# A transformer block pair at its start: the context columns as one array, the second token tile loaded directly behind the first, one square root for both

## The chip, the cores and the metric

The kernel runs on 1 core of one Trainium2 chip. The metric is the device time of one execution in microseconds (us). A core has TensorE (PE, with its weight loads PEld), VectorE (DVE), ScalarE (ACT), GpSimd (POOL) and SyncE (SP), which here only issues transfers.

## The reference

The inputs are x (8 batches of 100 tokens, 512 wide), a context ctx_512 (8 x 361 x 128) and the weights of two layers. In short:

```python
x = x + L0_xattn(layernorm(x), ctx_512, ...)   # 16 heads of 32, causal mask, softmax
x = x + L0_ffn(layernorm(x), ...)              # 8 experts, top 2 of them, silu gate
x = x + L1_xattn(layernorm(x), ctx_512, ...)   # latent attention with rotary tables
x = x + L1_ffn(layernorm(x), ...)              # rows rounded to 255 levels, silu gate

def L0_xattn(q, latent_kv, Wq, Wkv_expand, Wout):
    qp = q @ Wq.T
    k, v = jnp.split(latent_kv @ Wkv_expand.T, 2, axis=-1)
    ...
    scores = jnp.where(causal, scores, jnp.finfo(scores.dtype).min)
    attn = jax.nn.softmax(scores, axis=-1)
    ...
    return out @ Wout.T
```

The causal mask is lower triangular over 100 queries and 361 context rows, so that the first attention only ever sees the first 100 context rows of a batch. The change lies in the first attention alone.

## The kernel before

The 800 tokens lie in seven tiles of 128 rows (the last has 32), `xs[0]` to `xs[6]`. The kernel goes through the first attention batch by batch (0 to about 110 us), the choice of experts and the folding of some weights beside it (to about 140 us), the eight experts (to about 261 us), the second attention (to about 485 us) and the quantised feed-forward (to the end).

What the change touches is the start of the first attention, lines 193 to 288 and 465 to 475.

**Transfers.** At the start all are issued by SyncE, in the order in which they are written (L194 to L211, then the weights to be folded). They run on the same 16 DMA engines. `load_x(t)` brings one token tile, 256 KB. `wkv_sb` holds the weights of keys (first half) and values (second half), 256 KB each. `ctx0` holds the context's columns, 128 latent channels on the partitions and 8 x 100 rows along them, in two halves of four batches and 200 KB each (L198, L204). They are cut out of an array of 128 x 8 x 361 in HBM, so a partition's half is four pieces of 100 numbers (400 B). `wq_sb` holds the queries' weights, 1024 KB. The order before is x0, keys' weights, first context half, x1, wq, x2, x3, values' weights, second context half, x4 to x6, wout. From the ninth transfer on, each issue waits for the landing of the one eight places ahead of it, since eight semaphores are used in turn.

**Order of the engines.** From L249 TensorE, VectorE and ScalarE work in the order in which the program is written; nothing is moved by a scheduler there. An engine takes its instructions strictly in that order and waits at each for what it needs.

**The steps.** Three matmuls of zeros (L466) come first on TensorE. `first_norm(t0, t1)` takes mean and variance of the tiles t0 to t1-1 (L267, L268, VectorE), one square root over all of them (L271, ScalarE), one reciprocal (L272) and then a normalisation of each tile (L277), both on VectorE. `token_columns(t, xn)` transposes a tile's four blocks on TensorE (L286) and copies them to `xnT` (L287, ScalarE). `keys(h, o0, o1)` computes for four batches the key blocks o0 to o1-1 (L257, two passes each, TensorE) and copies them to `kT` (L261, ScalarE). `queries0(0, 2)` (L302, L306) needs the columns of tiles 0 and 1 and `wq_sb`. `first_norm(2, NT)` then treats the other five tiles together. `begin(0)` takes the scores of the first batch (L323, L329) and their maxima (L341, VectorE). The order before:

```python
    first_norm(0, 1)
    take_columns(0)
    first_norm(1, 2)
    keys(0, 0, 3)
    take_columns(1)
    keys(0, 3, KC)
    queries0(0, 2)
    first_norm(2, NT)
```

The first use of a function such as the square root on ScalarE is preceded by the loading of its table; this instruction is put in when the program is built and has the line of the instruction that it serves.

Of the kernel before, what the change touches and what calls it, by code (L numbers as in the profile page):

```python
# [19 lines left out]
P = 128  # L20
B, S, D = 8, 100, 512
N = B * S
L, DC = 361, 128
KC = D // P
# [26 lines left out]
def tile_kernel(  # L51
# [7 lines left out]
    nc = tc.nc  # L59
# [19 lines left out]
    def bank(dtype=F32):  # L79
        cols = 512 if dtype == F32 else 1024  # L80
        bank_turn[0] += 1
        pool = bank_pools[bank_turn[0] % len(bank_pools)]
        return pool.tile([P, cols], dtype, tag="bank", name="bank")
# [103 lines left out]
    ctx0 = ate.tile([P, B, S], F32, tag="ctx0", name="ctx0")  # L187
    wkv_sb = ate.tile([P, 2 * D], F32, tag="wkv", name="wkv_sb")
    wq_sb = ate.tile([P, KC, D], F32, tag="wq", name="wq_sb")
    xnT = ate.tile([P, KC, N], F32, tag="xnT", name="xnT0")  # L190
    wout_sb = at.tile([P, KC, D], F32, tag="wout", name="wout_sb")

    def load_x(t):
        nc.sync.dma_start(xs[t][: ROWS[t]], x[ds(t * P, ROWS[t]), :])  # L194

    load_x(0)
    nc.sync.dma_start(wkv_sb[:, :D], wkv0[:, :D])
    nc.sync.dma_start(ctx0[:, : B // 2], ctx_t[:, : B // 2, 0:S])  # L198
    load_x(1)
    nc.sync.dma_start(wq_sb, wq0.rearrange("(c p) o -> p c o", p=P))  # L200
    load_x(2)
    load_x(3)
    nc.sync.dma_start(wkv_sb[:, D:], wkv0[:, D:])
    nc.sync.dma_start(ctx0[:, B // 2 :], ctx_t[:, B // 2 :, 0:S])  # L204
    for t in range(4, NT):
        load_x(t)
    nc.sync.dma_start(wout_sb, wout0.rearrange("(c p) o -> p c o", p=P))
# [46 lines left out]
    def keys(h, o0=0, o1=KC):  # L254
        for o in range(o0, o1):
            pk = bank()
            nc.tensor.matmul(  # L257
                pk[:, :HALF], wkv_sb[:, ts(o, P)],
                ctx0[:, ds(h * 4, 4), :], start=True, stop=True,
            )  # L260
            nc.scalar.copy(kT[:, o, ts(h, HALF)], pk[:, :HALF])  # L261

    def token_stats(mvs, t0, t1):
        for t in range(t0, t1):
            r = ROWS[t]
            stats = small.tile([P, 6], F32, tag="stats", name="stats")
            nc.vector.bn_stats(stats[:r], xs[t][:r])  # L267
            nc.vector.bn_aggr(mvs[:r, t, :], stats[:r])  # L268

    def token_scales(mvs, sds, rstds, t0, t1):  # L270
        nc.scalar.activation(sds[:, t0:t1], mvs[:, t0:t1, 1], AF.Sqrt, bias=ln_eps)  # L271
        nc.vector.reciprocal(rstds[:, t0:t1], sds[:, t0:t1])  # L272

    def token_norm(t):
        r = ROWS[t]
        xn = ate.tile([P, D], F32, tag="xn0", name=f"xn0_{t}", bufs=NT)
        nc.vector.tensor_scalar(  # L277
            xn[:r], xs[t][:r], mv0[:r, t, 0:1], rstd0[:r, t : t + 1], ALU.subtract, ALU.mult
        )
        return xn  # L280

    def token_columns(t, xn):
        r = ROWS[t]
        pt = bank().rearrange("p (c q) -> p c q", c=KC)
        for c in range(KC):
            nc.tensor.transpose(pt[:, c, :r], xn[:r, ts(c, P)], ident[:r, :r])  # L286
        nc.scalar.copy(xnT[:, :, ds(t * P, r)], pt[:, :, :r])  # L287


    def queries0(b, n, parts=(0, 1)):  # L290
        per = 4 // n
        if parts[0] == 0:
            qT = atw.tile([P, KC, n * S], F32, tag=f"qT{n}", name=f"qT{b}")
            for i in range(n):
                queries_of[b + i] = qT[:, :, ts(i, S)]
                halves_of[b + i] = qT
        qT = halves_of[b]
        for o0 in [per * i for i in parts if per * i < KC]:
            pq = bank()
            for o in range(o0, o0 + per):  # L300
                for c in range(KC):
                    nc.tensor.matmul(  # L302
                        pq[:, ds((o - o0) * n * S, n * S)], wq_sb[:, c, ts(o, P)],
                        xnT[:, c, ds(b * S, n * S)], start=(c == 0), stop=(c == KC - 1),
                    )
            nc.scalar.activation(  # L306
                qT[:, ds(o0, per), :], pq[:, : KC * S].rearrange("p (c q) -> p c q", c=per),
                AF.Copy, scale=1.0 / math.sqrt(HD0),
            )
# [113 lines left out]
    queries_of, halves_of, soft, vals, xn0 = {}, {}, {}, {}, {}  # L423

    def first_norm(t0, t1):
        token_stats(mv0, t0, t1)
        token_scales(mv0, sd0, rstd0, t0, t1)
        for t in range(t0, t1):
            xn0[t] = token_norm(t)
# [5 lines left out]
    def take_columns(*tiles):  # L435
        for t in tiles:
            token_columns(t, xn0.pop(t))
# [26 lines left out]

    for _ in range(3):
        nc.tensor.matmul(bank()[:, :384], zeros[:, :P], zeros[:, :384], start=True, stop=True)  # L466
    first_norm(0, 1)
    take_columns(0)
    first_norm(1, 2)
    keys(0, 0, 3)  # L470
    take_columns(1)
    keys(0, 3, KC)
    queries0(0, 2)
    first_norm(2, NT)

# [533 lines left out]
    with tc.If(spills > 0, preferred_fallthrough_block=True):  # L1009
# [38 lines left out]
        with tc.For_i(0, NE, 1, hint_engines=()):  # L1048
# [12 lines left out]
            with tc.For_i(0, NT, 1, hint_engines=()):  # L1061
# [4 lines left out]
                pt = bank()  # L1066
# [661 lines left out]
    pt = bank()  # L1728
# [334 lines left out]
```

## Time and profile before

| what | us |
|---|---|
| the three timed runs | 624.87, 624.99, 627.96 (median 624.99) |
| the profiled execution | 624.9 |
| its span, from the first to the last instruction | 622.7 |
| TensorE busy in it | 601.0 (97%) |
| VectorE, ScalarE, GpSimd busy | 403.5, 231.8, 238.8 |

Times in the profile's rows count from the start of the span. A row of the order of time has start, duration, engine, line, operation, result and operands with their shape, and how many instructions were taken together; the brackets tell how long the engine had been idle before it and what ended that. SPq rows are issues of transfers, not the transfers. A row of the costliest groups has the count, the busy time in all and the mean in ns, then the idle time just before and what ended it. A row of waits has the total, the number and the longest.

These rows are the ones in which transfers are issued at the start (SPq), of which the prediction speaks:

```profile
0.79 0.39 SPq L194 DMA_DIRECT2D x<-in_x  x1
1.24 0.42 SPq L197 DMA_DIRECT2D wkv_sb<-in_wkv  x1
1.71 0.43 SPq L198 DMA_DIRECT2D ctx<-in_ctx_t  x1
2.18 0.51 SPq L194 DMA_DIRECT2D x<-in_x  x1
2.73 0.43 SPq L200 DMA_DIRECT2D wq_sb<-in_wq  x1
```

### The profile page before, as it was taken

What the parts mean: (1) busy time and instruction counts of PE and PEld (TensorE: products, weight loads), DVE (VectorE), ACT (ScalarE), POOL (GpSimd) and SP (SyncE); (2) the same over time, 40 slices, a digit from 0 to 9 for tenths busy, and PEclk for the clock granted to TensorE, in tenths of its full rate; (3) what the DMA queues carried; (4) which work ended last, traced back from release to release, by engine and by line L of the source; (5) the groups of instructions that cost most, each with busy time, mean ns of one, the idle gap of its engine ahead of it and who ended that gap; (6) DMA issues with size and microseconds to landing.
All of it is one profiled execution on the core that took longest, in us unless ns stands there. A gap on an engine that the chain in (4) does not pass through costs nothing.

```text
span 622.7 us, 12244 instructions
## 1 busy us (share of the span) xinstructions
PE 601.0 (97%) x4587; PEld 399.4 (64%) x4594; DVE 403.5 (65%) x1041; ACT 231.8 (37%) x533; POOL 238.8 (38%) x242
## 2 busy tenths in 40 slices
PE   8999999979999999999999999999999999999995
PEld 5767765647777777658877677777777544444442
DVE  4865778836777554253227888788874366766687
ACT  3553545561111111241336545556553121222130
POOL 1131231021333332208954868688685001222020
PEclk9999999999999999999999999999999999999998
DMA  8900096558999999773623332433210401110221
GB/s 279 326 20 35 2 298 182 179 155 255 306 301 268 233 329 308 201 197 102 180 67 86 91 101 53 127 88 88 59 50 6 139 10 32 24 31 11 53 41 68
DMA packets 92932, 83.75 MB, mean 134 GB/s; under 512 B 41195, under 2 KB 69567, under 8 KB 92743
## 3 DMA queue, kind: packets, MB, share of 16 engines
q1 hardware_dynamic: 88775, 73.57, 41.3%
q0 software_dynamic: 4096, 9.38, 7.3%
q8 instruction: 37, 0.61, 0.4%
q14 instruction: 24, 0.20, 0.1%
HBM read 63.75 MB, written 12.36 MB: 122 GB/s over the span
## 4 chain that ended last, share of the span: by engine, by line
PE 69%; DVE 5%; ACT 2%; issue 1%; POOL 1%; ACTq 0%; DVEq 0%
PE bank L390 13%; PE bank L1191 12%; PE four L1531 11%; PE bank L1497 8%; PE bank L1614 7%; PE bank L1252 7%; PE bank L1789 3%; PE bank L1292 2%; PE four L1461 2%; PE bank L1128 1%; PE four L1558 1%; ACT e L1505 1%; DVE sq L1522 1%; POOL hid L1806 1%; PE bank L396 1%
## 5 line engine op out<-in xcount | busy, mean ns | idle before, releaser
L1515 POOL TENSOR_SCALAR e<-e,rs 128x361 f32<-128x361 f32 x96 | 113.0, 1192 | 41.1 <-DVE rs L1511 40.8
L390 PE MATMUL bank<-wvo,ctxT 128*128 128x512 f32 x192 | 84.4, 594 | 0.0
L1505 ACT ACTIVATE e<-bank,nm 128x361 f32<-128x361 f32 x100 | 56.5, 567 | 51.6 <-DVE rs L1511 43.5
L1191 PE MATMUL bank<-xgT,w 128*128 128x240 f32 (+1 forms) x384 | 74.1, 369 | 0.4 <-ACT xgT L1132 0.4
L1191 PEld LDWEIGHTS bank<-xgT,w 128*128 128x128 f32 (+1 forms) x384 | 64.7, 181 | 11.5 <-issue 6.2
L1502 DVE TENSOR_REDUCE nm<-bank 128x1 f32<-128x361 f32 x100 | 50.8, 509 | 27.1 <-PE bank L1497 19.0
L1531 PEld LDWEIGHTS four<-sq,kv 32*128 32x128 f32 (+1 forms) x1536 | 62.2, 185 | 8.4 <-issue 4.8
L1497 PE MATMUL bank<-kvT,qe 128*128 128x361 f32 x192 | 67.3, 483 | 0.2
L1531 PE MATMUL four<-sq,kv 32*128 32x192 f32 (+1 forms) x1536 | 66.9, 325 | 0.0
L1806 POOL TENSOR_TENSOR hid<-g,u 128x512 f32<-128x512 f32 (+1 forms) x17 | 20.4, 1216 | 112.1 <-ACT g L1797 110.5
L390 PEld LDWEIGHTS bank<-wvo,ctxT 128*128 128x128 f32 x192 | 36.0, 190 | 42.5 <-issue 41.8
L1522 DVE STREAM_TRANSPOSE sq<-e 128x384 f32<-128x384 f32 x96 | 53.6, 558 | 1.6 <-POOL e L1515 0.8
L1264 POOL DMA_INDIRECT x_acc<-y,place x16 | 25.1, 1570 | 75.6 <-ACT y L1263 45.1
L355 POOL TENSOR_TENSOR s<-s,rs 100x800 f32<-100x800 f32 x16 | 24.4, 1522 | 70.3 <-DVE rs L354 35.5
L1497 PEld LDWEIGHTS bank<-kvT,qe 128*128 128x128 f32 x192 | 33.4, 189 | 22.6 <-issue 5.7
L1252 PE MATMUL bank<-w,hT 128*128 128x512 f32 (+3 forms) x96 | 42.6, 593 | 0.0
L1614 PE MATMUL bank<-xT,wqf 128*128 128x256 f32 (+1 forms) x128 | 31.2, 394 | 0.0
L1252 PEld LDWEIGHTS bank<-w,hT 128*128 128x128 f32 (+3 forms) x96 | 17.0, 183 | 19.7 <-issue 15.6
L1789 PE MATMUL bank<-w1q,xqT 128*128 128x512 bf16 (+1 forms) x140 | 29.2, 361 | 0.2
L1614 PEld LDWEIGHTS bank<-xT,wqf 128*128 128x128 f32 x128 | 23.8, 190 | 5.3 <-issue 0.5
L1794 DVE SCALAR_TENSOR_TENSOR g<-bank,sx,swb 128x512 f32<-128x512 f32 (+1 forms) x18 | 12.6, 702 | 19.0 <-PE bank L1789 18.5
L1202 ACT ACTIVATE silu<-bank 128x240 f32<-128x240 f32 x16 | 5.9, 370 | 50.1 <-PE bank L1191 50.1
(296 smaller groups left out, 961.5 us busy)
## 6 DMA issues: line engine op xcount, KB each, us to landing
w<-in_w SPq DMA_DIRECT2D x8, 1408.0 KB
gu<-in_wgu SPq DMA_DIRECT2D x22, 256.0 KB
wq_p<-in_wq SPq DMA_DIRECT2D x8, 512.0 KB
w<-in_w SPq DMA_DIRECT2D x16, 256.0 KB
wo<-in_wo SPq DMA_DIRECT2D x8, 512.0 KB
kq_p<-in_wkcq SPq DMA_DIRECT2D x16, 192.0 KB
kv<-ctx_rot SPq DMA_DIRECT2D x32, 96.0 KB
dn<-in_wdn SPq DMA_DIRECT2D x4, 704.0 KB
```

What stands on the lines that cost most here:

```text
L390: nc.tensor.matmul(po[:, :D], lhs[:, c, ds(t * P, r)], rhs[:, c, :], start=(c == 0), stop=(c == chunks - 1),)
L1191: nc.tensor.matmul(po, w12_e[:, c, cols], xgT[:, c, :], start=(c == c0), stop=(c == c1 - 1))
L1252: nc.tensor.matmul(py[i][:n], hT[:mr, m, ds(s0, n)], w3_e[:mr, m, :], start=(m == blocks[0]), stop=(m == blocks[2]),)
L1497: nc.tensor.matmul(ps[:, :L], of_batch(b)[a][:, h, s].rearrange("p g q -> p (g q)"), kvTs[b], start=True, stop=True,)
L1502: nc.vector.tensor_reduce(nm, ps[:, :L], AX.X, ALU.max, negate=True)
L1505: nc.scalar.activation(e[:, :L], ps[:, :L], AF.Exp, bias=nm, accum_out=sm)
L1515: nc.gpsimd.tensor_scalar_mul(e[:, :L], e[:, :L], rs)
L1522: nc.vector.transpose(squares[b, h][:, a * (HT // 2) + s, :], e)
L1531: nc.tensor.matmul(pc[:, g, :cols].rearrange("p (t q) -> p t q", q=32), kv4s[b, j // NBH][ds(32 * g, n), j % NBH, :], eT[ds(32 * g, n), :, ...
L1614: nc.tensor.matmul(pq[:, i, :], wqf[:, c, ts(p0 + i, P)], xT[:, c, :], start=(c == 0), stop=(c == KC - 1),)
L1789: nc.tensor.matmul(pw[:r, :n], xqT[:, c, :r], w1q[:, c, ds(off, n)], start=(c == 0), stop=(c == KC - 1),)
L1806: nc.gpsimd.tensor_tensor(hid[:r, ds(c0, n)], g[:r, :n], u[:r, :n], ALU.mult)
```

## The change

The host hands over the context's columns already cut to the first 100 rows of each batch, so that a half of `ctx0` is one run of 400 numbers (1600 B) on each partition of the array in HBM. The transfer of x1 stands directly behind that of x0. The means, variances and the square root of tiles 0 and 1 are taken together. On TensorE two key blocks now come first, then the transposes of both tiles, then the other two key blocks. The copy of the second tile's columns is done by VectorE.

```diff
--- before.py
+++ after.py
@@ -194,14 +194,14 @@
         nc.sync.dma_start(xs[t][: ROWS[t]], x[ds(t * P, ROWS[t]), :])
 
     load_x(0)
+    load_x(1)
     nc.sync.dma_start(wkv_sb[:, :D], wkv0[:, :D])
-    nc.sync.dma_start(ctx0[:, : B // 2], ctx_t[:, : B // 2, 0:S])
-    load_x(1)
+    nc.sync.dma_start(ctx0[:, : B // 2], ctx_t[:, : B // 2])
     nc.sync.dma_start(wq_sb, wq0.rearrange("(c p) o -> p c o", p=P))
     load_x(2)
     load_x(3)
     nc.sync.dma_start(wkv_sb[:, D:], wkv0[:, D:])
-    nc.sync.dma_start(ctx0[:, B // 2 :], ctx_t[:, B // 2 :, 0:S])
+    nc.sync.dma_start(ctx0[:, B // 2 :], ctx_t[:, B // 2 :])
     for t in range(4, NT):
         load_x(t)
     nc.sync.dma_start(wout_sb, wout0.rearrange("(c p) o -> p c o", p=P))
@@ -279,12 +279,12 @@
         )
         return xn
 
-    def token_columns(t, xn):
+    def token_columns(t, xn, copy=nc.scalar.copy):
         r = ROWS[t]
         pt = bank().rearrange("p (c q) -> p c q", c=KC)
         for c in range(KC):
             nc.tensor.transpose(pt[:, c, :r], xn[:r, ts(c, P)], ident[:r, :r])
-        nc.scalar.copy(xnT[:, :, ds(t * P, r)], pt[:, :, :r])
+        copy(xnT[:, :, ds(t * P, r)], pt[:, :, :r])
 
 
     def queries0(b, n, parts=(0, 1)):
@@ -464,12 +464,11 @@
 
     for _ in range(3):
         nc.tensor.matmul(bank()[:, :384], zeros[:, :P], zeros[:, :384], start=True, stop=True)
-    first_norm(0, 1)
-    take_columns(0)
-    first_norm(1, 2)
-    keys(0, 0, 3)
-    take_columns(1)
-    keys(0, 3, KC)
+    first_norm(0, 2)
+    keys(0, 0, 2)
+    token_columns(0, xn0.pop(0))
+    token_columns(1, xn0.pop(1), nc.vector.tensor_copy)
+    keys(0, 2, KC)
     queries0(0, 2)
     first_norm(2, NT)
 
@@ -2024,7 +2023,7 @@
     ordered = [
         ("x", a["x"].reshape(N, D)),
         ("ctx_n", a["ctx_512"]),
-        ("ctx_t", a["ctx_512"].transpose(2, 0, 1)),
+        ("ctx_t", a["ctx_512"][:, :S].transpose(2, 0, 1)),
         ("rope_cos", cos),
         ("rope_sin", sin),
         ("wq0", a["L0_xattn_Wq"].T),
```

## The prediction

> **What bounds the kernel now.** I read the page's first part, then the order of time of the first 20 us, then the waits and transfers of that stretch, because the diff touches nothing behind it.
>
> ```profile
> PE 601.0 (97%) x4587; PEld 399.4 (64%) x4594; DVE 403.5 (65%) x1041; ACT 231.8 (37%) x533; POOL 238.8 (38%) x242
> ```
>
> TensorE (PE) is busy for 97% of the span, so the kernel as a whole gives little. At its start TensorE still waits for rows, means and transfers. The next rows are start, duration, engine, line, operation, and in brackets the idle time before and who ended it:
>
> ```profile
> 0.79 1.28 ACT L271 ACT_TABLE_LOAD   x1 [0.79 <-PEq L2050]
> 3.59 0.69 DVE L267 BATCH_NORM_STATS2 stats<-x 128x6 f32<-128x512 f32 x1 [2.68 <-DMA x<-in_x]
> ...
> 4.40 0.18 DVE L268 BATCH_NORM_AGGREGATE mv<-stats 128x2 f32<-128x6 f32 x1
> ...
> 4.61 0.29 ACT L271 ACTIVATE sd<-mv,ln_eps 128x1 f32<-128x1 f32 x1 [2.54 <-DVE mv L268]
> 4.94 0.17 DVE L272 RECIPROCAL rstd<-sd 128x1 f32<-128x1 f32 x1 [0.36 <-ACT sd L271]
> 5.14 0.55 DVE L277 TENSOR_SCALAR xn<-x,mv,rstd 128x512 f32<-128x512 f32 x1
> ...
> 5.83 0.63 PE L286 MATMUL bank<-ident,xn 128*128 128x128 f32 x4 [0.49 <-DVE xn L277]
> ...
> 6.60 2.25 PE L257 MATMUL bank<-ctx,wkv_sb 128*128 128x400 f32 x6
> 7.58 0.69 DVE L267 BATCH_NORM_STATS2 stats<-x 128x6 f32<-128x512 f32 x1 [1.90 <-DMA x<-in_x]
> ...
> 9.66 0.66 PE L286 MATMUL bank<-ident,xn 128*128 128x128 f32 x4 [0.80 <-DVE xn L277]
> ...
> 10.35 0.58 ACT L287 COPY xnT<-bank 128x512 f32<-128x512 f32 x1 [0.36 <-PE bank L286]
> ...
> 10.99 5.68 PE L302 MATMUL bank<-xnT,wq_sb 128*128 128x200 f32 x32
> ...
> 17.11 0.29 ACT L271 ACTIVATE sd<-mv,ln_eps 128x5 f32<-128x5 f32 x1
> ...
> 17.65 2.36 DVE L277 TENSOR_SCALAR xn<-x,mv,rstd 128x512 f32<-128x512 f32 x5
> ...
> 19.94 0.56 DVE L341 TENSOR_REDUCE mx<-bank 100x4 f32<-100x400 f32 x1
> ```
>
> The reader is to see four things. The square root's table is loaded at 0.79, while ScalarE has nothing else to do. The second token tile is not there until 7.58. TensorE stands idle for 0.80 us before its transposes. The queries (L302) begin at 10.99, behind the second tile's copy (10.35 + 0.58 = 10.93). From there the path is plain: queries to 16.67, their second evacuation to 17.21, the square root of the other five tiles, their norms, and only then the first maximum of the scores at 19.94. The list of waits from 16 to 100 us names no transfer at all, so I take a shift of the queries' start to be passed on whole to the end. **The quantity to forecast is when L302 begins.**
>
> Transfers decide part of it. The trace also keeps when each of the sixteen pieces of a transfer lands. First and last piece, in us: x0 3.16 and 3.57; keys' weights 3.85 and 4.21; context half 4.77 and 6.47; x1 5.58 and 7.56; wq 8.56 and 10.73. SyncE's own list has the last one too, as its next issue stood waiting for it until 10.75:
>
> ```profile
> SPq L207 <- DMA wq_sb<-in_wq: 2.5, 1, 2.5
> ```
>
> **The change, part by part.**
>
> x1 earlier: it takes the queue place of the keys' weights, of the same 256 KB and the same row size, so I put its landing at 4.21, 3.35 us earlier. VectorE (DVE) is free for it at 4.58 + 0.03.
>
> One square root for both tiles: this takes away one square root, one reciprocal and their hops (some 0.65 us), and puts the first tile's normalisation behind the second tile's statistics. Statistics at 4.61, 0.69; aggregate at 5.33, 0.18, to 5.51. **A wait is added here that the diff does not show.** In the built instruction list ScalarE's first square root has two awaited engines now (VectorE, whose results it reads, and POOL, whose memset wrote the same tile). The wait for VectorE's second aggregate stands as an instruction of its own *ahead of the table load*. Before, the table load stood first and waited for nothing. The trace of before has the same construction at L1797, with the table load idle until VectorE:
>
> ```profile
> L1797 ACT ACT_TABLE_LOAD x4 | 5.1, 1283 | 32.5 <-DVE g L1794 32.5
> ```
>
> So 1.28 us that were free at 0.79 go on the path: table load 5.55 to 6.83, square root at 6.85. With the hops of the rows above (square root to reciprocal 0.33, to normalisation 0.20, to transposes 0.69): reciprocal 7.18, normalisations 7.38 to 7.93 and to 8.45, transposes from 8.07. Queued behind that wait on ScalarE are the keys' copies, the first tile's copy and the queries' copies. The earliest of them is wanted at about 7, so nobody else waits for it.
>
> TensorE's work, unchanged in amount: two keys, eight transposes, two keys. A key takes two passes 0.335 apart (1.34 for two keys), transposes 0.11 each (eight in 1.04 with their tail, row at 19.97). If the norms decide: first tile 8.07 to 8.5, second from 8.55 to 9.0, two keys to 10.34, queries at **10.35**. The second tile's copy moves to VectorE; its nearest row (L621, a bank of 128x512 to SBUF) is 0.69, so it lies from about 9.2 to 9.9, beside the keys. Behind it VectorE has the statistics of x2, which waited for their transfer until 11.42 anyway. If that cover goes, the copy costs its 0.69.
>
> Whole pieces for the context: 400 B pieces become 1600 B ones. I have no row of 1600 B; the nearest is x1 at 2048 B. By its pace (0.81 us for 256 KB on the fastest engine) 200 KB take 0.63 instead of 0.92, so 0.29 us saved; the bounds are no saving and, if the small pieces made the slow engines slow, the whole lag of 1.7 us. The context is now fourth in the queue. Its last piece lands at 5.3 (no lag) to 7.27 (x1's 7.56 less 0.29). Keys first in TensorE's order means that the transposes wait for this landing K: queries at K + 0.1 + 1.34 + 0.9 + 1.34 = K + 3.7, that is 9.0 to 10.95. wq, the fifth, lands at 10.44 by the same saving, and TensorE can use it at about **10.5**.
>
> The start is the latest of 10.35, K + 3.7 and 10.5. I take K near the middle of its bounds (6.3), which leaves wq and the norms as the limit: 10.5 to 10.55, against 10.99, a gain of **0.45 us**. What is late next: the statistics of x4 to x6 end at 16.65 and their square root now could start at 17.21 - 0.45 - 0.1 = 16.66, so the gain just fits without those tiles coming sooner; beyond it they have to (two halves of the context, 0.29 each, move them).
>
> The lane waits of SyncE (its ninth to twelfth transfers wait for the first four) change places only; all are over by 7.6. The context's array in HBM shrinks from 1.48 to 0.41 MB, so all arrays behind it lie elsewhere; no row prices that, and I give it nothing.
>
> Against the profiled execution's 624.9 us (span 622.7 and 2.2 around it; the median of the three runs is 624.99, the same): 624.9 - 0.45 = **624.5 us**.
>
> [...] Rows first: at L348 the table load starts at 20.78, within 0.02 us of the copy before it, and at L786 the copy starts 0.02 us after the load, so a switch costs 1.28 us here. [...]
>
> **Rivals.**
>
> 1. *Slower: the context is late.* Keys stand ahead of the transposes on TensorE, and the context stands behind x1 in the queue. For it: the third to fifth transfers had slow pieces 1.7 to 2.2 us behind the fast ones. It decides from K = 7.3 (10.99 - 3.7). If the context has x1's slow landing and then its own old 0.92, K is 8.2 to 8.5 and the queries begin at 11.9 to 12.2: +0.9 to +1.2, **626.0**. Against it: larger pieces.
> 2. *No gain.* K at 7.27 or wq at its old 10.73 leaves 10.85 to 11.0: 624.8 to **624.9**. For it: bytes ahead of wq are the same.
> 3. *The table load stays hidden, or the lag of the slow engines goes with the 400 B pieces.* Without the load the norm branch is 9.07; without lag wq lands at 8.3 and K is 5.3. The queries could begin at 9.4, but the statistics of x4 to x6 then hold the square root; with those tiles 0.3 to 1.4 sooner the gain is 0.8 to 1.6, **623.7**. Against: L1797.
> 4. *The shift is not passed on, or the arrays' new places in HBM matter:* a microsecond or more either way.
>
> **How the numbers follow.** Forecast (gain of 0.2 to 0.7) 0.48; no gain 0.20; context late 0.15; larger gain 0.08; the rest 0.09. The range reaches from rival 3's far end to rival 1's: 624.9 - 1.6 = 623.3, and 624.9 + 1.2 = 626.1; the three runs of before differ by 3.1 us among themselves, so I leave it no narrower than 623.2 to 626.2. Half a per cent, about what a measurement of this kernel can tell from no change, is 3.1 us, and none of the first three rivals comes near: only the last case gives chances beyond it, faster 0.04, slower 0.06, so 0.90 within.
>
> **What would show it.** Right: x1's statistics start near 4.6; the table load starts at about 5.55 with idle time ended by VectorE; L302 starts at 10.3 to 10.7; the first maximum comes some 0.45 earlier than 19.94. Wrong: a table load at 0.8; keys starting after 7.3; L302 after 11; or a first maximum that moves while the end does not.

## The result and the profile after

| | before | changed |
|---|---|---|
| median of 22 runs each, us | 624.91 | 626.9 |
| lowest and highest, us | 623.01, 633.77 | 624.75, 634.71 |
| profiled execution and its span, us | 624.9, 622.7 | 626.23, 624.5 |

The ratio is 1.0043, with a 95% interval of 1.0025 to 1.0061: the changed kernel is slower by some 1.6 to 3.8 us. Medians here are over all runs; ratios leave out those more than 1.5% above the fastest of their kernel.

TensorE's work has not grown by a single instruction (4594 weight loads before and after; of the matmuls of before 4587 are recorded), yet the first line of the page (share of the span, instructions) counts 3.4 us more of busy time than the 601.0 of before. The same matmuls took longer:

```profile
PE 604.4 (97%) x4594; PEld 400.6 (64%) x4594; DVE 403.8 (65%) x1041; ACT 231.5 (37%) x531; POOL 239.1 (38%) x242
```

The order of time of the changed kernel's first 21 us, with the columns as in the prediction's rows:

```profile
4.52 0.66 DVE L267 BATCH_NORM_STATS2 stats<-x 128x6 f32<-128x512 f32 x1
...
5.48 1.28 ACT L271 ACT_TABLE_LOAD   x1 [5.48 <-DVE mv L268]
...
6.63 3.00 PE L257 MATMUL bank<-ctx,wkv_sb 128*128 128x400 f32 x4 [0.91 <-DMA ctx<-in_ctx_t]
6.78 0.29 ACT L271 ACTIVATE sd<-mv,ln_eps 128x2 f32<-128x2 f32 x1
...
7.30 1.00 DVE L277 TENSOR_SCALAR xn<-x,mv,rstd 128x512 f32<-128x512 f32 x2
...
9.43 1.28 PE L286 MATMUL bank<-ident,xn 128*128 128x128 f32 x8
...
10.54 1.51 PE L257 MATMUL bank<-ctx,wkv_sb 128*128 128x400 f32 x4
10.74 0.69 DVE L287 COPY xnT<-bank 128x512 f32<-128x512 f32 x1 [2.44 <-PE bank L286]
...
11.89 5.58 PE L302 MATMUL bank<-xnT,wq_sb 128*128 128x200 f32 x32
...
20.73 0.56 DVE L341 TENSOR_REDUCE mx<-bank 100x4 f32<-100x400 f32 x1
```

The row to look at is the third. Its four passes took 3.00 us, while four passes of the same shape took 1.51 at 10.54: TensorE ran at half pace. The bracket shows what came before, 0.91 us of idle time until the context landed. The row at 7.30 takes both tiles' normalisations together, so the first was ready at about 7.8; its transposes began at 9.43 nevertheless, for the keys stand ahead of them. The queries started at 11.89 instead of 10.99, and the first maximum moved from 19.94 to 20.73, by +0.79.

The trace also records when TensorE's full clock is granted and withdrawn. Before, it was granted at 4.83 us and kept to 619.23. In the changed kernel it was granted at 9.91, withdrawn at 136.20 and granted again at 139.62. The second loss is visible in a table of time stretches (TensorE's busy time, instructions, granted clock, transfer share, GB/s), first of the changed kernel:

```profile
134.00:136.00 2.00, 0.57 (x5) 1.00 0.71 205
136.00:138.00 2.00, 2.00 (x6) 0.55 0.11 29
138.00:140.00 2.00, 2.00 (x9) 0.60 0.46 124
```

and the same stretches of the kernel before:

```profile
134.00:136.00 2.00, 1.05 (x7) 1.00 0.64 182
136.00:138.00 2.00, 1.47 (x9) 1.00 0.03 8
138.00:140.00 2.00, 1.80 (x16) 1.00 0.80 229
```

There the fold's eight matmuls (L791; L792 before) take 3.48 us instead of 1.94. Just ahead of them, the fold's transposes began at 134.48 instead of 133.96: of the 0.90 us at the queries and the 0.79 at the first maximum, 0.52 was left. The first matmul of the experts is at 141.76 instead of 140.18 (+1.58), and the span ends 1.81 later. So the time was lost in two places, both through the clock: at the start, and at 136 us, in a stage that the diff doesn't touch, which in this pair of profiles lost the more.

### The profile page after: what moved, and what is told of

Same layout as the page of the kernel before. It is cut to its first block, busy times and chain, and to the rows that moved or that the text cites. A ratio compares the mean times of both kernels' runs of the same rounds, so it can differ in the third digit from the quotient of the medians.

```text
span 624.5 us, 12249 instructions
## 1 busy us (share of the span) xinstructions
PE 604.4 (97%) x4594; PEld 400.6 (64%) x4594; DVE 403.8 (65%) x1041; ACT 231.5 (37%) x531; POOL 239.1 (38%) x242
## 4 chain that ended last, share of the span: by engine, by line
PE 47%; DVE 5%; issue 3%; ACT 2%; DMA 2%; POOL 1%; ACTq 0%; SPq 0%; DVEq 0%; POOLq 0%
PE bank L390 13%; PE four L1530 11%; PE bank L1496 8%; PE bank L1613 7%; PE bank L1788 3%; PE four L1460 2%; DMA x_acc<-y,place 1%; PE four L1557 1%; ACT e L1504 1%; DVE sq L1521 1%; POOL hid L1805 1%; PE bank L396 1%; DVE y L1917 1%; PE bank L1301 1%; PE bank L1491 0%
```

## The experiments

**Theory**, a supposition from the two profiles. When TensorE's full clock is granted (4.83 us before, 9.91 in the changed kernel) depends on how busy TensorE was just before. Before, transposes follow the zeros after 0.49 us; now the keys do, after 0.91, and they wait for a transfer. The idle time delays the grant, and up to it TensorE runs at half pace, as in the keys' 3.00 us against 1.51. **Rivals:** the context is simply late (rival 1 of the prediction); the table load on the norm's path costs the time; the new places of transfers or arrays do.

**More zeros, to close the gap.** One more zero matmul in the changed kernel covers part of the wait with activity:

```diff
-    for _ in range(3):
+    for _ in range(4):
```

> The changed kernel with four matmuls of zeros at the start in place of three. Clock theory: the changed kernel lost because TensorE stood idle from 5.72 to 6.63 us, so the stretch of activity that releases its clock was broken and the clock came at 9.91 instead of 4.83. Four zeros last to about 6.4 to 6.9 us and close that gap; the clock is then granted by 8.3 us at the latest, L302 begins at 10.4 to 10.9 and the median falls to within 0.5 us of before (0.998 to 1.001). Table theory (1.28 us of table load on the path) and late-context theory: nothing changes, 1.003 to 1.005, L302 near 11.9.

Ratio 1.0008 (0.9976 to 1.0039). Its order of time:

```profile
6.74 1.58 PE L257 MATMUL bank<-ctx,wkv_sb 128*128 128x400 f32 x4 [0.77 <-DMA ctx<-in_ctx_t]
...
8.16 1.04 PE L286 MATMUL bank<-ident,xn 128*128 128x128 f32 x8
9.04 1.51 PE L257 MATMUL bank<-ctx,wkv_sb 128*128 128x400 f32 x4
...
10.38 5.58 PE L302 MATMUL bank<-xnT,wq_sb 128*128 128x200 f32 x32
...
19.23 0.56 DVE L341 TENSOR_REDUCE mx<-bank 100x4 f32<-100x400 f32 x1
```

With the context landing at about the same time (6.74), the keys run at 1.58 instead of 3.00, and the queries begin at 10.38, 1.51 us earlier. The clock was granted at 4.81. The profile shows what an early clock is worth, but not that the fourth zero brought it: the clock came while the zeros were still running, and 0.77 us of idle time was left in front of the keys. At 134.51 the clock was withdrawn for 3.4 us all the same.

**The table load back to the start.** Here ScalarE does a square root that nobody uses before everything else; the table is then loaded at 0.79.

```diff
+    early = at.tile([P, 1], F32, tag="early", name="early")
+    nc.scalar.activation(early, ln_eps, AF.Sqrt)
```

> The changed kernel with a square root of a constant into a spare tile ahead of everything on ScalarE, so that the table is loaded at 0.8 us as before. Table theory: the real square root starts at about 5.5 and L302 some 0.9 to 1.3 us earlier than in the changed kernel, ratio to before 1.001 to 1.002. Clock theory: normalised rows are ready at about 7 but TensorE still does its keys at half clock until 9.4, so L302 stays within 0.2 us of 11.9 wherever the clock comes as late, ratio 1.003 to 1.005.

Ratio 1.0046 (1.0011 to 1.0081), no gain. From its order of time (three lines were added, so L257 is L260 and L302 is L305 there):

```profile
7.59 1.58 PE L260 MATMUL bank<-ctx,wkv_sb 128*128 128x400 f32 x4 [1.87 <-DMA ctx<-in_ctx_t]
...
11.22 5.58 PE L305 MATMUL bank<-xnT,wq_sb 128*128 128x200 f32 x32
```

The norm was indeed ready earlier (6.94), but the keys waited until 7.59 and the queries began at 11.22, which is the prediction's K + 3.7. Taking away the table load gives nothing in this execution, as the keys' wait for the context ends later. One thing goes against the theory as it stands: the zeros are those of the changed kernel and the idle time is longer (1.87 us), and yet the clock was granted at 6.24 and the keys ran at full pace. The last section takes this up.

**Five zeros, and five zeros with the early table.**

> The changed kernel with five matmuls of zeros at the start in place of three: they last to about 6.4 us where the clock comes at 4.8, to 7.9 us where it stays away that long, so TensorE has no gap before its keys. Clock theory: the clock is granted once and kept through the first 20 us; L302 at 10.3 to 11.0; about half of the runs have a granted clock of 0.997 or more, as those of before have, where the changed kernel had none in 22; ratio to before 0.998 to 1.001. Late-context theory (the transposes wait behind the keys, whatever the clock does): still 1.003 to 1.005.

> Five matmuls of zeros and the square root of a constant first on ScalarE, so that neither gap nor table load is left. Clock theory with the table load as the next limit: normalised rows at 7.0 instead of 8.3, L302 at 9.6 to 10.6 by the context's landing, ratio 0.997 to 1.000, some 0.5 us under five zeros alone. Table theory: 1 us or more under five zeros alone. Late-context theory: no better than five zeros.

Ratios 1.0017 (0.9986 to 1.0049) and 1.003 (0.9989 to 1.0071). Both profiles have the clock at the start (granted at 4.83 and 5.84), keys at 7.61 and 7.43, queries at 11.25 and 11.07: again K + 3.64, with the table load on the path or off it. The ratios lie above those that the theory forecast. Between 131 and 142 us the first profile then loses the clock twice for 3.4 us, the second once for 10.2.

**Wider zeros.** Three zero matmuls of 512 columns instead of 384:

> The changed kernel with its three matmuls of zeros 512 instead of 384 columns wide, so that they last to about 6.0 to 6.6 us: the gap is closed as with four zeros, by another edit and with the same bank order as in the changed kernel. Clock theory: 0.999 to 1.002, clock granted by 7.3 at the latest and L302 at max(10.4, landing of the context + 3.7), so 10.4 to 11.3. Late-context and table theories: 1.003 to 1.005.

Ratio 1.0047 (1.0008 to 1.0086), above the forecast. The profile has the start mended (keys 1.58 us long, queries at 10.32), but the twelve runs spread from 624.57 to 633.8, four of them at 624.6 to 624.8. The whole kernel's times don't separate the start from what comes later.

**The two halves of the change in the whole kernel.** First whole pieces alone, in the kernel before:

```diff
-    nc.sync.dma_start(ctx0[:, : B // 2], ctx_t[:, : B // 2, 0:S])
+    nc.sync.dma_start(ctx0[:, : B // 2], ctx_t[:, : B // 2])
```

(the same for the second half, and the cut by the host).

> The kernel before with the context's array cut by the host and loaded in whole 1600 B pieces, nothing else changed. Clock theory: no new gap on TensorE, so no loss; 0.999 to 1.001, L302 at 10.7 to 11.0, held by the second tile's landing. If the new places of the arrays in HBM are what costs, it is slower by the whole 0.4%.

Ratio 1.0001 (0.9967 to 1.0034). The profiled execution is the shortest of the whole kernel's (span 621.8), and its start is faster by 1.05 us, in the order of time:

```profile
6.53 0.69 DVE L267 BATCH_NORM_STATS2 stats<-x 128x6 f32<-128x512 f32 x1 [0.93 <-DMA x<-in_x]
...
9.94 5.68 PE L302 MATMUL bank<-xnT,wq_sb 128*128 128x200 f32 x32
```

x1, directly behind the context in the queue, is usable at 6.53 instead of 7.58; `wq_sb` must have been there by 9.94. Neither the runs nor the other profiles (see the last section) show a gain that can be told from none.

Then x1 behind x0 as well, with the engines' order of before:

```diff
     load_x(0)
+    load_x(1)
     nc.sync.dma_start(wkv_sb[:, :D], wkv0[:, :D])
-    nc.sync.dma_start(ctx0[:, : B // 2], ctx_t[:, : B // 2, 0:S])
-    load_x(1)
+    nc.sync.dma_start(ctx0[:, : B // 2], ctx_t[:, : B // 2])
```

> The kernel before with the transfers of the changed one (x1 directly behind x0, whole pieces of context), its engines' order and its two square roots as before. Clock theory: TensorE's gap stays 0.5 us long as the first tile's transposes come at 5.8, the clock is kept, L302 at 9.4 to 10.3, ratio 0.997 to 1.000, half the runs at a granted clock of 0.997 or more. If the transfers' order or the arrays' places cost the time, 1.003 to 1.005.

Ratio 0.9992 (0.9953 to 1.0032), with the clock from 6.15 and the queries at 10.37. And the new order of the engines with x1 where it was:

```diff
     load_x(0)
-    load_x(1)
     nc.sync.dma_start(wkv_sb[:, :D], wkv0[:, :D])
     nc.sync.dma_start(ctx0[:, : B // 2], ctx_t[:, : B // 2])
+    load_x(1)
```

> The changed kernel with x1 put back behind the first context half: the new order on the engines and the whole pieces, but not the early second tile. Context lands at about 6.2 and x1 at 6.5; table load behind the shared statistics to 8.8, transposes at about 10, L302 at 11.5 to 12, and a second gap on TensorE of two us between keys and transposes. Clock theory and table theory: slower than the kernel before, 1.002 to 1.006, few runs with a granted clock of 0.997 or more. If the transfers' order is what costs: 0.999 to 1.001.

Ratio 1.0052 (1.0027 to 1.0078): the loss goes with the engines' order. In its order of time the keys are not late, and are still slow:

```profile
6.28 3.01 PE L257 MATMUL bank<-ctx,wkv_sb 128*128 128x400 f32 x4 [0.55 <-DMA ctx<-in_ctx_t]
7.81 1.28 ACT L271 ACT_TABLE_LOAD   x1 [7.81 <-DVE mv L268]
...
10.33 1.06 PE L286 MATMUL bank<-ident,xn 128*128 128x128 f32 x8 [1.05 <-DVE xn L277]
```

**The kernel before with fewer and more zeros, and the changed kernel once more.**

> The kernel before with two matmuls of zeros in place of three: TensorE's first stretch ends at about 4.1 us and it idles until 5.8. Clock theory: the clock is released late (at 7 us or after) although order, transfers and table load are those of before, and the kernel is slower by 0.5 to 2 us, 1.001 to 1.004, with a tail. The other theories: nothing changes, 0.999 to 1.001.

> The kernel before without any matmul of zeros, the large dose: TensorE's first work is the first tile's transposes at 5.8, so the clock cannot come before about 8.2 and comes by 11.6. Clock theory: keys take 0.67 per pass instead of 0.335, L302 at 11.5 to 13.5, ratio 1.003 to 1.006. Table and late-context theories: no change, 0.999 to 1.001, L302 at 11.

> The kernel before with the context in whole pieces and four matmuls of zeros: the candidate for a version that beats both. The fourth runs into the first tile's transposes and the keys (context at about 6.2), so TensorE has no gap before 8.5. Clock theory: L302 at 9.9 to 10.6, the clock kept through the first 20 us, 0.997 to 1.000. If the zeros only delay what follows, 1.000 to 1.001.

> The changed kernel once more, unedited, beside the three others on the same chip. Clock theory: ratio 1.002 to 1.006, no run with a granted clock of 0.997 or more, and a profile in which the clock either comes late (after 6.5 us) or is withdrawn again within the first 10 us. If the loss were a matter of single runs, the ratio would fall to 1.000 to 1.002 and half of the runs would have 0.997 or more.

Two zeros: 1.0037 (1.0007 to 1.0068), though its profile has the clock from 4.61, not late as forecast, behind 1.34 us of idle time, and the queries at 11.06. No zeros: 1.0013 (0.9984 to 1.0041), with the clock from 11.54 and the queries at 12.21; the 8.2 and 11.6 of its forecast are estimates, one and two steps of 3.413 us (last section) behind before's 4.83. Pieces with four zeros: 1.0012 (0.9982 to 1.0041). The changed kernel again: 1.0015 (0.9973 to 1.0057); its profile has the keys at 7.20 behind 1.48 us of idle time, 3.01 us long, the clock from 10.63, the queries at 12.53 and the end 3.13 later than before's. The keys are slow in both profiles of the changed kernel (3.00 and 3.01 us, with the clock from 9.91 and 10.63), but not every gap makes the clock late (1.87 us with the early table, 1.34 with two zeros); the ratios do not order as the starts do. A difference of 1 to 2 us at the start can't be read from whole executions, because the stage near 135 us gives or takes as much.

**The start by itself.** So I ended the kernel behind the first five batches of the first attention, at L508; the four runs of the kernel before then agree within 0.3 us. The first two are the kernel before and the changed kernel, the others those with four zeros and with the early table, with the diffs shown above; all ran on one chip.

> The kernel before cut off behind the first five batches of the first attention (it writes the token tiles as they then stand; the last two batches and all later layers are left out). It is the yardstick for three others cut the same way, so that the stage from 127 to 141 us, where the clock is withdrawn at random, cannot blur the head. About 80 us, runs within 1 us of one another if the head is steady.

> The changed kernel cut off in the same place (last two batches and all later layers left out). Clock theory: 0.5 to 1.5 us slower in the median than the cut kernel before, spread over two groups, one with the clock early (0 to 0.5 us faster), one with it late (1 to 2 us slower). If the loss comes behind the head, the two cut kernels are the same within 0.3 us or this one is faster.

> The changed kernel with four matmuls of zeros, cut off in the same place (last two batches and all later layers left out). Clock theory: 0.7 to 1.5 us under the cut changed kernel and at or under the cut kernel before. Late-context theory: as the cut changed kernel, within 0.3 us.

> The changed kernel with the square root's table loaded first, cut off in the same place (last two batches and all later layers left out). Table theory: 0.7 to 1.3 us under the cut changed kernel. Clock and late-context theories: within 0.3 us of it, since the keys are in TensorE's way until the context has landed.

| cut kernel | median, us | runs, us |
|---|---|---|
| before | 81.50 | 81.41 to 81.68 |
| changed | 83.26 | 82.92 to 83.65 |
| changed, four zeros | 81.59 | 81.37 to 82.42 |
| changed, early table | 82.04 | 81.70 to 82.19 (four), 83.86 and 84.00 |

The changed start costs **1.76 us**, and one zero matmul of no use gives back 1.67 of them; the four runs of the one and of the other do not overlap. The group with an early clock that was forecast for the changed one did not appear. The waits of the cut changed kernel (total, number, longest) name its gap:

```profile
PE bank L257 <- DMA ctx<-in_ctx_t: 1.8, 1, 1.8
```

and its order of time the price, the clock being granted at 10.30:

```profile
7.49 2.97 PE L257 MATMUL bank<-ctx,wkv_sb 128*128 128x400 f32 x4 [1.82 <-DMA ctx<-in_ctx_t]
...
10.29 1.05 PE L286 MATMUL bank<-ident,xn 128*128 128x128 f32 x8
...
12.52 5.58 PE L302 MATMUL bank<-xnT,wq_sb 128*128 128x200 f32 x32
```

With four zeros, the profiled execution being the slowest of its four:

```profile
7.96 1.58 PE L257 MATMUL bank<-ctx,wkv_sb 128*128 128x400 f32 x4 [1.39 <-DMA ctx<-in_ctx_t]
...
11.60 5.58 PE L302 MATMUL bank<-xnT,wq_sb 128*128 128x200 f32 x32
```

In the cut kernel before they began at

```profile
10.17 5.68 PE L302 MATMUL bank<-xnT,wq_sb 128*128 128x200 f32 x32
```

With four zeros the context is later by 0.47 us than in the changed kernel, yet the queries begin 0.92 earlier: with the clock (granted at 6.06) they come 3.64 us after the keys begin, without it 5.03. That is the separation wanted. Of the 2.35 us from 10.17 to 12.52 the half pace makes 1.39; the other 0.96 goes with the context's landing at 7.49 (7.49 + 3.64 = 11.13). Both cost time in these executions, the half pace the more, and the one with four zeros was still 1.01 us longer than the profiled one of before (82.42 against 81.41). How the 1.76 us between the medians divide is not shown, as the other runs have no profile.

The early table is 1.22 us under the changed kernel in the median, which is what the table theory had forecast. Two of its six runs are as long as the changed kernel's, and in the profile of the 84.00 run the clock came at 10.95; the group near 81.8 I take, without a profile of it, for runs in which it came in time. So a share of the table load isn't excluded. Against a large one: with four zeros the load is still on the path (5.32 to 6.60), and the loss is gone.

**The two halves in the cut kernel.**

> The changed kernel with x1's transfer back behind the first context half, cut off behind the first five batches of the first attention (the last two batches and all later layers are left out). The cut kernel before took 81.5 us, the cut changed one 83.26. Theory (keys, which wait for the context, stand directly behind the zeros, so the clock is granted late): the new order of the engines alone brings the loss, whatever place x1 has: 82.6 to 83.6 us, TensorE idle for over 0.5 us between zeros and keys, clock granted after 9 us. Rival (x1's place ahead of the context makes the context late, and that is the loss): with the context early again the keys start by 6.4 and the cut kernel takes 81.2 to 81.8.

> The kernel before with x1's transfer directly behind x0's and the context in whole pieces, its order of the engines kept; cut off in the same place (the last two batches and all later layers are left out). Theory: the first tile's transposes still follow the zeros after 0.1 to 0.5 us, the clock is granted by 6.5, and nothing is lost; x1 earlier brings up to 0.6 us: 80.9 to 81.6 us against 81.5. Rival (the transfers make the loss): 82.6 to 83.6 us.

Both ran on one other chip. The new order of the transfers: 81.66 us (81.45 to 81.78), as good as before's 81.50 and without the gain that was forecast. The new order of the engines: 84.06 us, six runs at 82.35, 82.91, 83.28 and 84.85, 85.02, 85.07; all lie above the other's. The loss goes with the engines' order; but x1 comes late here, and the norms with it, so this is not the changed kernel's loss by itself. That the second group lies beyond the theory's 83.6 has a cause which its profile (of the 84.85 run) shows:

```profile
5.62 2.52 PE L257 MATMUL bank<-ctx,wkv_sb 128*128 128x400 f32 x4
...
10.06 1.14 PE L286 MATMUL bank<-ident,xn 128*128 128x128 f32 x8 [1.93 <-DVE xn L277]
11.00 2.88 PE L257 MATMUL bank<-ctx,wkv_sb 128*128 128x400 f32 x4
```

```profile
9.00:10.00 1.00, 0.00 (x0) 1.00 1.07 411
10.00:11.00 1.00, 0.94 (x9) 0.96 1.04 392
11.00:12.00 1.00, 1.00 (x4) 0.50 1.13 397
12.00:13.00 1.00, 1.00 (x2) 0.50 1.01 322
```

Here the keys followed the zeros without a gap, as the context was there at 5.62, and the clock was granted at 7.50. Then TensorE stood for 1.93 us until the late norms came, and the clock was withdrawn at 10.92, 3.42 us after its grant, until 14.33: now it is the *second* pair of keys that takes 2.88 us. The other two runs of the group have the same mean granted clock, 0.98. My theory had named one gap, between zeros and keys; here a later one, of 1.93 us, came ahead of a loss of the clock.

## Why the prediction was wrong

The prediction said 624.5 us with a range of 623.2 to 626.2; measured is 626.9.

- **x1 earlier, one square root:** right. x1's statistics began at 4.52 (said: near 4.6).
- **The wait hidden in the built program:** right in its mechanism. The table load started at 5.48 (5.55) behind VectorE, the normalisations at 7.30 (7.38). That the queries came at 10.38 and 10.32 with four and with wider zeros, next to the 10.35 of the norm branch, is a coincidence: both are K + 3.64, set by the keys, as in the profiles with a later context. In the whole kernel nothing was gained without the load; in the cut kernel its share stays open.
- **The copy on VectorE:** right, 0.69 us beside the keys.
- **K, the landing of the context:** mis-sized. I took 6.3; the keys that waited for it began at 6.63 in the profile after and, over the twelve profiles with x1 moved up, at 6.63 to 7.96 with a median of 7.3, six of them beyond the upper bound of 7.27. By the prediction's own K + 3.7 this is no gain, rival 2. Where the new order of the engines had the clock early and kept it, this is what happened: K + 3.6 six times (10.32, 10.38, 11.07, 11.22, 11.25, 11.60), and the cut kernel with four zeros is as fast as the cut kernel before.
- **wq at 10.5 as the limit:** too late; it was used at 9.94 with whole pieces alone.
- **The step that failed** is the sum along TensorE: "A key takes two passes 0.335 apart (1.34 for two keys), transposes 0.11 each". I took durations that TensorE has at the granted clock and used them behind a wait. I asked of the wait between the zeros and K only how long it is, not what it does to the work behind it. Measured in the profile after: two keys 3.00, not 1.58, and transposes at K + 2.8 instead of K + 1.4. With its K of 6.63 the prediction's own K + 3.7 gives 10.33; the half pace makes the 1.56 us from there to 11.89. In the cut kernel the start costs 1.76 us in place of a gain of 0.45.
- **Everything behind the start** was put at nothing, and a shift was to be passed on whole. In the profiles 0.90 us at the queries had become 0.52 at 134 us, and the stage near 136 us, at half pace, made it 1.58.
- **Rival 1** had the right sign and named the wait, with a wrong price: it decided from K = 7.3 on, but the queries began at 11.89 and 12.53 at K = 6.63 and 7.20. That its 626.0 lies close to the measured time is luck. The clock was in the trace's records (the page's second part, in slices of 15.6 us, has the same 9 at the start before and after), and I never asked what had earned its grant at 4.83.

What the table load cost on ScalarE is its own 1.28 us: the square root starts at 6.78, 0.02 us after the load ends at 6.76.

**What stays open.** The loss near 136 us is seen in the profiles of all variants of the whole kernel with the new order of the engines, and in one without it (the new order of the transfers alone). Counting runs whose granted clock was 0.997 or more, which leaves room for one stretch of 3.413 us at half pace at most (see the last section), the end included (the profile before has 0.997 with the clock at half from 619.23 to its end at 622.7 alone): 0 of 22 and 1 of 12 for the changed kernel, 14 to 18 of 35 for the kernel before in the runs beside the experiments, 8 of 12 with whole pieces alone, but also 5 of 12 with five zeros and the early table, 4 of 12 with four zeros, 3 of 12 with the engines' order alone and 1 of 12 with the transfers' order alone. So this loss does not go with the engines' order alone. In that stage TensorE stands twice for about a microsecond (1.20 and 0.95 us) in the profiles before and after and in most others. In the changed kernel the 3.413 us ahead of the withdrawal (132.79 to 136.20) hold both, and TensorE is busy for 1.26 us of them, 37%; in the kernel before, whose clock stayed, two steps counted from its grant share them, with 2.16 us (131.11 to 134.53) and 1.99 us (134.53 to 137.94), 63 and 58%. Why the changed kernel meets the loss more often is open. The start's 1.76 us lies inside the whole kernel's interval of 1.6 to 3.8 us, though the changed kernel's second measurement (1.0015) can't be told from no loss; how much the later stage adds to it on average isn't settled.

## What to carry to other kernels

Before a matmul that waits for a transfer is put at the head of TensorE's queue, ask what the idle time does to the clock: durations taken from rows at full clock may not hold behind a wait. Here the keys' four passes took 3.00 us behind 0.91 us of idle time, and 1.58 behind 0.77 with four zeros. Work that is ready, or even matmuls of zeros for as long as the wait can last, belongs in front of it; here one more of them gave back 1.67 us of the cut kernel. And where whole executions scatter by more than the effect, cut the kernel behind the stage and time that: 1.76 us in 83 was plain, in 625 it was not.

## What the runs showed of the hardware

**In these records the clock changed in steps of 3.413 us.** In the changed kernel the withdrawal lies 126.29 us after the first grant, 37.0 times 3.413, and the next grant 3.413 after that; in the kernel before, the clock was kept for 614.40 us, 180.0 times 3.413; in the engines-only cut the changes are at 7.50, 10.92 and 14.33. The records have two values: 1.00 from a grant and 0.50 from a withdrawal, as from 136.20 to 139.62 in the changed kernel. The passes agree: the keys' four took 3.00 us ahead of the grant and 1.51 behind it. Below, a window is a stretch of 3.413 us, counted in such steps from the first grant.

**In these profiles the clock went with how full a window was.** The length of a gap alone does not decide. With 0.91 us of idle time the grant came at 9.91, and 1.93 us in the engines-only cut preceded a withdrawal; but with the same zeros and 1.87 us the clock came at 6.24 (the early table in the whole kernel). What the records fit better is a share, TensorE's busy time summed over one window:

| profile | window that ended at | TensorE busy | clock |
|---|---|---|---|
| before | 4.83 | 97% | first granted |
| changed | 6.50 | 77% | not yet granted |
| changed | 9.91 | 96% | first granted |
| early table | 6.24 | 85% | first granted |
| two zeros | 4.61 | 86% | first granted |
| cut changed | 6.88 | 64% | not yet granted |
| cut changed | 10.30 | 82% | first granted |
| changed | 136.20 | 37% | withdrawn |
| four zeros | 134.51 | 48% | withdrawn |
| engines-only cut | 10.92 | 44% | withdrawn |
| before | 137.94 | 58% | kept |

From the first grant to the last microseconds, the profiles before and after kept the clock after every other window, and none of those was less than 58% busy. The two sides of the grant overlap. With the engines' order alone in the whole kernel, all four passes of the keys were slow to 9.29 and the transposes at 10.33 were not, which puts the grant between 9.2 and 10.4, an estimate from these rows. The window before that one's had no idle time but the 0.55 us ahead of the keys, so it was 84% busy or more and earned nothing, where 82% did in the cut changed kernel. The matmuls' ends are modelled, so these shares are rough, and a bound can't be read from them.

By this reading it matters where the windows lie against the kernel's start, and that differed between executions: windows ended at 6.24, 6.50 and 6.88, and three zeros and then a wait earned the clock in the first and not in the other two. An estimate from these rows says what the fourth zero does: at half pace it lasts 1.40 us (4.21 for three), to about 7.1, and would have filled both windows that failed, those that ended at 6.50 and at 6.88. It didn't have to close the gap: with four zeros 0.77 us of idle time was left in the whole kernel and 1.39 in the cut one, and the clock came at 4.81 and 6.06.

**An effect of whole pieces isn't shown.** With 1600 B pieces in place of 400 B ones, x1, the next transfer in the queue, was usable 1.05 us sooner (6.53 against 7.58). But over the profiles with x1 behind the context its statistics began at 6.43, 6.91, 7.42 and 7.58 with 400 B pieces and at 6.53, 6.55, 6.82 and 7.73 with 1600 B ones: the two overlap.
